# Starting layer 1's first chunk beside the last chunk of layer 0

## The chip, the cores and the metric

The kernel runs on one core of a Trainium2 chip. The metric is the device time of one execution in microseconds (us). The engines are TensorE (PE, with its weight loads PEld), VectorE (DVE), ScalarE (ACT), GpSimd (POOL) and SyncE (SP, which here only issues DMAs).

## The reference

Two layers work on x of 16 sequences x 256 tokens x 256 features, all in float32. Cut to what matters here:

```python
xn = layernorm(x)                             # layer 0
y  = recurrent_scan(xn) @ C + D * xn          # 32 complex states, along the tokens
z  = silu(gelu(xn @ proj1.T + b1) @ proj2.T + b2)
x  = x + y * z
xn = layernorm(x)                             # layer 1
q  = xn @ Wq                                  # 16 heads, 128 plain + 64 rotated features
kv = xn @ Wkv_a                               # 64 latent + 64 rotated features
c  = rmsnorm(kv[..., :64]) * kv_norm_w
k, v = split(c @ Wkv_b)                       # k is joined with the rotated part of kv
s  = causal_softmax(q @ k.T / sqrt(192)) @ v @ Wo
mid = (xn @ lora_A) * gate                    # 8 experts x 16; gate: softmax of the best two router logits
z  = silu(xn @ base_w.T + base_b + 2 * mid @ lora_B)
x  = x + s * z
```

## The kernel before

The 4,096 tokens are worked in 8 chunks of 512 tokens (two sequences); X[ch] stays on the chip through both layers. Layer 0 goes over all chunks first, then layer 1.

**Layer 0** is the loop `for ch in range(NCH)` (line 560). For each chunk: `hidden` (PE matmuls ph, ACT Gelu to hT), `recur` (PE pb, then a chain on DVE and POOL to hs), `norm0` and `turn0` of the next chunk (PE transposes tp, copies to xnT), `mix(ch, 0)` (32 matmuls pf, DVE add and ACT Silu to zf), `outs` (PE py, DVE dx), `finish0(ch, 0)` (POOL: dx times zf, then added to X), `mix(ch, 1)` and `finish0(ch, 1)` for the other half. In the last chunk there is no next chunk, so nothing stands between pb and the first pf. PSUM is held in pools `ps_mm` (4 buffers), `ps_y` (2) and `ps_f` (2).

**Layer 1** starts after the pools of layer 0 are given back (line 593); its own pools lie in the memory of layer 0, so an instruction that writes into them waits for the last user of the place. Its first steps, in lines 1002 to 1027, work on chunk 0:

- `norm_begin` and `norm_end` (lines 621 and 634): 4 bn_stats, 4 bn_aggr and one tensor_scalar on DVE, a power on POOL (rs), 4 tensor_scalar on DVE (xn).
- `transpose_chunk` (643): 8 PE transposes tp, 2 copies on ACT to xnT.
- `kv_begin`, `kv_end`, `key_chunk` (652 to 692): 8 matmuls pkv, an ACT Square, a chain on DVE and POOL (tmp, ss, rk, row), 4 transposes pk and a copy to kT, the keys.
- `router_chunk` (693): 8 matmuls pm, then some 20 small DVE operations (lg to gate) with one ACT Exp, and the gated product mid.
- the queries of the first two groups of four heads. `query_mm` makes pq on PE, `query_mul` multiplies the rotated part on DVE (qmul), `query_rot` adds it up on POOL (qrot), `query_move` sends it with 8 DMAs of SP to the query tile qg, `query_lat` writes the plain part to qg on ACT.

Then the loop over units (line 1033; one unit is a group of four heads of one sequence, 8 units to a chunk) writes `score_pack` (PE sc, DVE mask and maxima nm, ACT Exp to pr), `normalise` (DVE reciprocals sr, POOL product pr), `turn` and `send` (DVE transposes to turned, 4 DMAs to far), `fetch` (a DMA to pT), `values` (av), and among them the queries of later groups and the same steps norm to router for chunk ch + 1. The norm of the next chunk stands in units 0 and 2 of the chunk (lines 1096 and 1053).

The probabilities of a unit lie in one of two tiles `prs`, which are cleared at their making by two POOL memsets (lines 802 to 804).

Order: `pe` is a wrapper that keeps PE's instructions in the order of the text; in layer 1 so do `sp`, `ve`, `ac` and `gp` for the others. In layer 0 most DVE, ACT and POOL instructions are placed by the scheduler, with respect to data only. So the instructions of layer 1 may move ahead of instructions of layer 0, but not past each other: the norm of chunk 0, whose X is complete early, ran at 152.88 us on DVE.

The layer norm adds its scale to each instruction like this, which makes xn wait for rs of POOL:

```python
gp.tensor_tensor(k.rs, v, mhalf, ALU.pow)
...
    ve.tensor_scalar(
        k.xn[:, j, :], X[ch][:, j, :], k.mv[:, j, 0:1], k.rs[:, j : j + 1],
        ALU.subtract, ALU.mult,
    )
```

Of the kernel before, what the change touches and what calls it, by code (L numbers as in the profile page):

```python
# [40 lines left out]
def tile_two_layers(ctx: ExitStack, tc: tile.TileContext, d: dict, out: bass.AP):  # L41
# [153 lines left out]
    def bc_in(ap, n):  # L195

        return ap.unsqueeze(2).to_broadcast([ap.shape[0], ap.shape[1], n])


    with ExitStack() as l0:  # L200
# [359 lines left out]
        for ch in range(NCH):  # L560
            if ch > 1:
                hT = hidden(ch, xnT)
            if ch == 0:

                xnT2 = turn0(1, xn2)
                zf = [mix(ch, jp, hT) for jp in range(2)]
                hT = hidden(1, xnT2)
                turn_b()
                g = recur(ch, xnT)
                fold_heads(ch)  # L570
                g0_, xn0, zf0 = g, xn, zf
            else:
                g = recur(ch, xnT)
                if ch < NH // HG:
                    fold_heads(ch)
                if ch == 1:
                    zf = mix(ch, 0, hT)
                    dx = outs(0, g0_, xn0)
                    for jp in range(2):
                        finish0(0, jp, dx, zf0[jp])  # L580
                if ch + 1 < NCH:
                    xn2 = norm0(ch + 1)
                    xnT2 = turn0(ch + 1, xn2)
# [18 lines left out]

    sp = InOrder(nc.sync)
    ve = InOrder(nc.vector)
    ac = InOrder(nc.scalar)
    gp = InOrder(nc.gpsimd)
    ps_m1 = ctx.enter_context(tc.tile_pool(name="ps_m1", bufs=5, space=PSUM))
    ps_sc = ctx.enter_context(tc.tile_pool(name="ps_sc", bufs=3, space=PSUM))

    def m1(name, shape):  # L610
        return ps_m1.tile(shape, F32, tag="m1", name=name)

    class Chunk:
        pass

    chunks = [Chunk() for _ in range(NCH)]
    for k in chunks:
        k.attT, k.po = [], {}


    def norm_begin(ch):
        k = chunks[ch]
        st = sm.tile([P, TPC, 6], F32, tag="ln_st", name=f"st_1_{ch}")
        k.mv = sm.tile([P, TPC, 2], F32, tag="ln_mv", name=f"mv_1_{ch}")
        v = sm.tile([P, TPC], F32, tag="ln_ve", name=f"ve_1_{ch}")
        k.rs = sm.tile([P, TPC], F32, tag="ln_rs", name=f"rs_1_{ch}")
        for j in range(TPC):
            ve.bn_stats(st[:, j, :], X[ch][:, j, :])
        for j in range(TPC):
            ve.bn_aggr(k.mv[:, j, :], st[:, j, :])  # L630
        ve.tensor_scalar(v, k.mv[:, :, 1], LN_EPS, None, ALU.add)
        gp.tensor_tensor(k.rs, v, mhalf, ALU.pow)

    def norm_end(ch):
        k = chunks[ch]
        k.xn = x1.tile([P, TPC, D], F32, tag="xn", name=f"xn1_{ch}", bufs=1)
        for j in range(TPC):
            ve.tensor_scalar(
                k.xn[:, j, :], X[ch][:, j, :], k.mv[:, j, 0:1], k.rs[:, j : j + 1],
                ALU.subtract, ALU.mult,  # L640
            )

    def transpose_chunk(ch):
        k = chunks[ch]
        k.xnT = x1.tile([P, 2, CH], F32, tag="xnT", name=f"xnT1_{ch}")
        for c in range(2):
            ps = m1(f"tp_1_{ch}_{c}", [P, CH])
            for j in range(TPC):
                pe.transpose(ps[:, j * P : (j + 1) * P], k.xn[:, j, c * P : (c + 1) * P], ident)
            ac.copy(k.xnT[:, c, :], ps)  # L650

    def kv_begin(ch):

        k = chunks[ch]
        k.pkv = pkv = m1(f"pkv_{ch}", [P, TPC, P])
        for j in range(TPC):
            for c in range(2):
                pe.matmul(
                    pkv[:, j, :], k.xnT[:, c, j * P : (j + 1) * P], wkva[:, c, :],
                    start=(c == 0), stop=(c == 1),  # L660
                )
        k.row = a2.tile([P, TPC, P], F32, tag="row", name=f"row_{ch}")
        k.tmp = tmp = a2.tile([P, 3, TPC, KVL], F32, tag="tmp", name=f"tmp_{ch}", bufs=1)
        sq, ra, rb = tmp[:, 0], tmp[:, 1], tmp[:, 2]
        ss = sm.tile([P, TPC], F32, tag="ss", name=f"ss_{ch}")
        k.rk = sm.tile([P, TPC], F32, tag="rk", name=f"rk_{ch}")
        ac.activation(sq, pkv[:, :, 0:KVL], AF.Square)
        x1_ = pkv[:, :, KVL : KVL + HR]
        x2_ = pkv[:, :, KVL + HR : P]
        ve.tensor_tensor(ra[:, :, 0:HR], x1_, rope_k[:, 0], ALU.mult)  # L670
        ve.tensor_tensor(ra[:, :, HR:ROPE], x2_, rope_k[:, 0], ALU.mult)
        ve.tensor_tensor(rb[:, :, 0:HR], x2_, rope_k[:, 1], ALU.mult)
        ve.tensor_tensor(rb[:, :, HR:ROPE], x1_, rope_k[:, 2], ALU.mult)
        ve.tensor_reduce(ss, sq, AX.X, ALU.add)
        ve.tensor_scalar(ss, ss, 1.0 / KVL, RMS_EPS, ALU.mult, ALU.add)
        gp.tensor_tensor(k.rk, ss, mhalf, ALU.pow)
        gp.tensor_tensor(k.row[:, :, KVL:P], ra, rb, ALU.add)

    def kv_end(ch):
        k = chunks[ch]  # L680
        sq = k.tmp[:, 0]
        ve.tensor_tensor(sq, k.pkv[:, :, 0:KVL], bc_in(k.rk, KVL), ALU.mult)
        ve.tensor_tensor(k.row[:, :, 0:KVL], sq, bc(kvw_bc, TPC), ALU.mult)

    def key_chunk(ch):
        k = chunks[ch]
        pk = m1(f"pk_{ch}", [P, CH])
        for j in range(TPC):
            pe.transpose(pk[:, j * P : (j + 1) * P], k.row[:, j, :], ident)
        k.kT = a2.tile([P, CH], F32, tag="kT", name=f"kT_{ch}")  # L690
        ac.copy(k.kT, pk)

    def router_chunk(ch):

        k = chunks[ch]
        lg = sm.tile([P, TPC, NE], F32, tag="lg", name=f"lg_{ch}")
        mid = a2.tile([P, TPC, P], F32, tag="tmp", name=f"mid_{ch}", bufs=1)
        for jp in range(2):
            pm = m1(f"pm_{ch}_{jp}", [P, 2, 256])
            for j2 in range(2):  # L700
                j = 2 * jp + j2
                for c in range(2):
                    pe.matmul(
                        pm[:, j2, 0 : P + NE], k.xnT[:, c, j * P : (j + 1) * P], wmid[:, c, :],
                        start=(c == 0), stop=(c == 1),
                    )
            ve.tensor_tensor(
                lg[:, 2 * jp : 2 * jp + 2, :], pm[:, :, P : P + NE], bc(rb_bc, 2), ALU.add
            )
            ac.copy(mid[:, 2 * jp : 2 * jp + 2, :], pm[:, :, 0:P])  # L710

        def t3(name):
            return sm.tile([P, TPC, NE], F32, tag=name, name=f"{name}_{ch}")

        def t2(name):
            return sm.tile([P, TPC], F32, tag=name, name=f"{name}_{ch}")

        def first_max(l, n, between=None):

            m, fm, eq, oh = t2(f"m{n}"), t2(f"fm{n}"), t3(f"eq{n}"), t3(f"oh{n}")  # L720
            ve.tensor_reduce(m, l, AX.X, ALU.max)
            if between:
                between(m)
            ve.tensor_tensor(eq, l, bc_in(m, NE), ALU.is_equal)
            ve.tensor_tensor(eq, eq, desc, ALU.mult)
            ve.tensor_reduce(fm, eq, AX.X, ALU.max)
            ve.tensor_tensor(oh, desc, bc_in(fm, NE), ALU.is_equal)
            return m, oh

        ex = t3("ex")  # L730

        def exps(m):
            ve.tensor_tensor(ex, lg, bc_in(m, NE), ALU.subtract)
            ac.activation(ex, ex, AF.Exp)

        _, oh1 = first_max(lg, 1, exps)
        l2 = t3("l2")
        ve.scalar_tensor_tensor(l2, oh1, -3e38, lg, ALU.mult, ALU.add)
        _, oh2 = first_max(l2, 2)
        ve.tensor_tensor(oh1, oh1, oh2, ALU.add)  # L740
        ve.tensor_tensor(ex, ex, oh1, ALU.mult)
        sw = t2("sw")
        ve.tensor_reduce(sw, ex, AX.X, ALU.add)
        ve.reciprocal(sw, sw)
        ve.tensor_scalar(sw, sw, LORA_SCALE, None, ALU.mult)
        gate = t3("gate")
        ve.tensor_tensor(gate, ex, bc_in(sw, NE), ALU.mult)
# [451 lines left out]
```

## Time and profile before

| | us |
|---|---|
| median of 3 runs | 968.23 |
| lowest and highest of the runs | 966.02, 969.03 |
| the profiled execution | 970.78 |
| its span, first to last instruction | 969.0 |
| PE busy in the span | 934.6 |
| DVE, ACT, POOL busy | 617.5, 427.7, 421.5 |
| end of the last pf of layer 0 | 285.76 |
| first score matmul of layer 1 | 306.35 |

Lines of instructions have the start in us, the length in us, the engine, the line of the kernel (L52 is the wrapper's line, common to all that go through it), the operation, the tile written <- the tiles read, the shape and the count; in brackets the idle time of the engine before it and what ended it. Lines of waits have who waited for whom, the total in us, the times and the longest. Lines of stretches have the stretch, its length, the busy time of PE, PEld, DVE, ACT and POOL with instruction counts, the mean clock that was granted to PE (1.00 is full), the share and the rate of the DMAs.

### The profile page before, as it was taken

The page shows a single profiled execution, that of the slowest core. Times are in us where ns is not written, and L with a number is a line of the kernel's source. Part 1 is how long each engine was busy: PE and PEld are TensorE (multiplying, and loading weights), DVE is VectorE, ACT ScalarE, POOL GpSimd, SP SyncE. Part 2 cuts the span into 40 slices and gives each one's busy share as a digit, 9 for nine tenths or more (in the row PEclk, how much of TensorE's full clock was granted, in tenths as well). Part 3 has the DMA queues.
Part 4 walks back from the last instruction along what each step waited for, and adds up shares of the span by engine and source line. Part 5 has one row for each costly group of instructions (what it writes and reads, how often), then busy time and mean ns, then how long its engine had stood idle before and what let it go on. Part 6 is the DMA issues. An engine that isn't in the chain of part 4 may idle for free.

```text
span 969.0 us, 15714 instructions
## 1 busy us (share of the span) xinstructions
PE 934.6 (96%) x4762; PEld 670.7 (69%) x4762; DVE 617.5 (64%) x1942; ACT 427.7 (44%) x1422; POOL 421.5 (43%) x751
## 2 busy tenths in 40 slices
PE   4989999999999999999999999999999999999988
PEld 3847557756675566777777777777777776777776
DVE  6776415321236968867876786786788679677562
ACT  2331332233324546544554464555456455446540
POOL 3115334223233445553645455455446544546440
PEclk9989999999999989999999999999999999999999
DMA  9503000000002577777777677678667767867860
GB/s 312 173 5 105 0 1 1 1 0 1 1 0 37 121 199 186 208 189 188 190 186 201 168 169 224 158 191 202 171 166 210 201 171 183 209 166 190 221 192 29
DMA packets 195941, 133.90 MB, mean 138 GB/s; under 512 B 142160, under 2 KB 186512, under 8 KB 195856
## 3 DMA queue, kind: packets, MB, share of 16 engines
q1 hardware_dynamic: 192864, 127.18, 50.5%
q0 software_dynamic: 1376, 3.67, 1.0%
q10 hardware_dynamic: 1616, 2.04, 0.7%
q8 instruction: 39, 0.64, 0.3%
q14 instruction: 46, 0.38, 0.1%
HBM read 63.11 MB, written 52.95 MB: 120 GB/s over the span
## 4 chain that ended last, share of the span: by engine, by line
PE 87%; DVE 6%; POOL 2%; DMA 2%; ACT 1%; issue 1%; SPq 1%; ACTq 0%; POOLq 0%; DVEq 0%
PE pq L52 22%; PE sc L52 14%; PE po L52 10%; PE ph L52 10%; PE pf L52 9%; PE av L52 9%; PE pg L52 4%; PE pm L52 2%; PE pkv L52 1%; PE tp L52 1%; PE pb L52 1%; PE psq L52 1%; PE py L52 1%; DMA x<-in_x_dram 1%; SPq L52 1%
## 5 line engine op out<-in xcount | busy, mean ns | idle before, releaser
L52 ACT ACTIVATE pr<-sc,nm 128x256 f32<-128x256 f32 (+7 forms) x512 | 189.5, 380 | 287.3 <-DVE sr L52 197.4
L52 POOL TENSOR_SCALAR pr<-pr,sr 128x256 f32<-128x256 f32 (+7 forms) x512 | 192.2, 394 | 276.2 <-DVE sr L52 273.3
L52 PEld LDWEIGHTS sc<-kT,qg 128*128 128x128 f32 x1024 | 161.1, 192 | 64.5 <-issue 40.2
L52 PE MATMUL sc<-kT,qg 128*128 128x256 f32 (+7 forms) x1024 | 177.9, 308 | 6.1 <-DMA qg<-qrot 4.2
L52 DVE STREAM_TRANSPOSE turned<-pr 128x512 f32<-128x512 f32 x186 | 123.3, 688 | 15.1 <-POOL pr L52 14.9
L52 DVE TENSOR_REDUCE nm<-sc 128x1 f32<-128x256 f32 (+7 forms) x512 | 127.7, 301 | 6.6
L52 PE MATMUL pq<-xnT,wlat 128*128 128x512 f32 x256 | 124.4, 609 | 0.0
L52 PE MATMUL pq<-xnT,wrope 128*128 128x512 f32 x256 | 120.1, 592 | 0.0
L52 PE MATMUL ph<-xnT,p1T 128*128 128x512 f32 (+1 forms) x288 | 114.8, 558 | 3.6 <-ACT xnT L52 3.2
L52 PE MATMUL po<-wout,attT 128*128 128x256 f32 x512 | 115.8, 380 | 0.0
L52 PE MATMUL pf<-p2T,hT 128*128 128x256 f32 x512 | 113.9, 381 | 0.0
L52 PEld LDWEIGHTS po<-wout,attT 128*128 128x128 f32 x512 | 96.4, 190 | 20.9 <-issue 6.4
L52 PEld LDWEIGHTS pf<-p2T,hT 128*128 128x128 f32 x512 | 96.1, 190 | 15.5 <-issue 1.8
L52 ACT ACTIVATION_READ_ACCUMULATOR pr<-sc,nm 128x1 f32 x512 | 103.6, 202 | 0.0
L52 PEld LDWEIGHTS ph<-xnT,p1T 128*128 128x128 f32 x288 | 56.6, 197 | 57.4 <-issue 48.6
L52 PE MATMUL av<-pT,row 128*64 128x256 f32 (+1 forms) x1024 | 90.5, 329 | 0.5 <-DMA pT<-far 0.5
L52 POOL TENSOR_TENSOR qrot<-qmul,qmul 128x512 f32<-128x512 f32 x64 | 83.0, 1317 | 15.3 <-DVE sc L52 9.9
L52 DVE TENSOR_TENSOR qmul<-pq,rot_q 128x512 f32<-128x512 f32 x128 | 80.9, 674 | 0.0
L52 PEld LDWEIGHTS av<-pT,row 128*64 128x64 f32 x1024 | 64.2, 137 | 23.3 <-PE av L52 0.8
L52 DVE TENSOR_TENSOR sc<-sc,kmask 128x96 f32<-128x96 f32 (+1 forms) x192 | 45.9, 239 | 52.1 <-PE sc L52 50.7
L52 ACT ACTIVATE qg<-pq 64x512 f32<-64x512 f32 x128 | 75.4, 589 | 6.8 <-PE pq L52 6.0
L52 PEld LDWEIGHTS pq<-xnT,wlat 128*128 128x128 f32 x256 | 46.2, 193 | 32.2 <-issue 32.1
(166 smaller groups left out, 910.4 us busy)
## 6 DMA issues: line engine op xcount, KB each, us to landing
far<-turned SPq DMA_DIRECT2D x248, 192.0 KB, 3.6
pT<-far SPq DMA_DIRECT2D x62, 768.0 KB, 4.6
qg<-qrot SPq DMA_DIRECT2D x256, 64.0 KB, 2.3
x<-in_x_dram SPq DMA_DIRECT2D x7, 512.0 KB, 9.1
out_dram<-o POOLq DMA_DIRECT2D x28, 128.0 KB, 3.2
wqn<-in_wq_nopeT_dram SPq DMA_DIRECT2D x4, 512.0 KB, 5.2
wo<-in_Wo_dram SPq DMA_DIRECT2D x4, 512.0 KB, 5.3
p1T<-in_proj1T_dram ACTq DMA_DIRECT2D x2, 512.0 KB, 4.8
```

Source lines behind the costliest of these rows:

```text
L52: r = getattr(self.engine, name)(*args, **kw)
```

## The change

The definitions of layer 1's steps move ahead of layer 0, unchanged but for the pools that they take. The pools `sm1`, `x1` and a new `ak` (row, tmp, kT and mid) are opened in front of both layers and so share no memory with layer 0. `m1` takes PSUM from the pool in `place`: from `ps_mm` of layer 0 while the last chunk runs, from `ps_m1` afterwards. In the last chunk of layer 0 the steps of layer 1's chunk 0, and the norm of its chunk 1, are written between those of layer 0; they are taken out of the places where they stood.

```diff
+    sm1 = ctx.enter_context(tc.tile_pool(name="sm1", bufs=2))
+    x1 = ctx.enter_context(tc.tile_pool(name="x1", bufs=2))
+    ak = ctx.enter_context(tc.tile_pool(name="ak1", bufs=2))
...
+    place = {}
+
+    def m1(name, shape):
+        return place["pool"].tile(shape, F32, tag=place["tag"], name=name)
...
         for ch in range(NCH):
             if ch > 1:
                 hT = hidden(ch, xnT)
+            if ch == NCH - 1:
+                place.update(pool=ps_mm, tag="mm")
+                norm_begin(0)
+                norm_end(0)
...
+                last = ch == NCH - 1
+                if last:
+                    transpose_chunk(0)
+                    kv_begin(0)
                 if ch > 1:
                     zf = mix(ch, 0, hT)
+                if last:
+                    kv_end(0)
+                    key_chunk(0)
                 dx = outs(ch, g, xn)
                 finish0(ch, 0, dx, zf)
+                if last:
+                    router_chunk(0)
                 zf = mix(ch, 1, hT)
                 finish0(ch, 1, dx, zf)
+                if last:
+                    norm_begin(1)
+                    norm_end(1)
             xn, xnT = xn2, xnT2
...
-    sm = ctx.enter_context(tc.tile_pool(name="sm1", bufs=2))
-    x1 = ctx.enter_context(tc.tile_pool(name="x1", bufs=2))
+    place.update(
+        pool=ctx.enter_context(tc.tile_pool(name="ps_m1", bufs=5, space=PSUM)), tag="m1"
+    )
...
-    norm_begin(0)
-    norm_end(0)
     ve.tensor_scalar(bb_bc, bb_bc, 0.5, None, ALU.mult)
-    transpose_chunk(0)
-    kv_begin(0)
     query_mm(0, 0)
     query_mul(0, 0)
     query_mm(0, 1)
-    kv_end(0)
     query_mul(0, 1)
     query_rot(0)
     query_move(0)
-    key_chunk(0)
     query_mm(0, 2)
     query_lat(0, 2)
     query_mm(0, 3)
     query_lat(0, 3)
-    router_chunk(0)
...
-            if more:
+            if more and ch:
                 norm_end(ch + 1)
...
-        if r == 0 and more:
+        if r == 0 and more and ch:
             norm_begin(ch + 1)
```

More of the change, by code (lines that the diff above doesn't have):

```diff
@@ L197, in bc_in @@
         return ap.unsqueeze(2).to_broadcast([ap.shape[0], ap.shape[1], n])
+    sm1 = ctx.enter_context(tc.tile_pool(name="sm1", bufs=2))
+    x1 = ctx.enter_context(tc.tile_pool(name="x1", bufs=2))
+    ak = ctx.enter_context(tc.tile_pool(name="ak1", bufs=2))
+    sp = InOrder(nc.sync)
+    ve = InOrder(nc.vector)
+    ac = InOrder(nc.scalar)
+    gp = InOrder(nc.gpsimd)
+    place = {}
+    def m1(name, shape):
+        return place["pool"].tile(shape, F32, tag=place["tag"], name=name)
+    class Chunk:
+        pass
@@ new lines, in tile_two_layers, with norm_begin @@
+    chunks = [Chunk() for _ in range(NCH)]
+    for k in chunks:
+        k.attT, k.po = [], {}
+    def norm_begin(ch):
+        k = chunks[ch]
+        st = sm1.tile([P, TPC, 6], F32, tag="ln_st", name=f"st_1_{ch}")
+        k.mv = sm1.tile([P, TPC, 2], F32, tag="ln_mv", name=f"mv_1_{ch}")
+        v = sm1.tile([P, TPC], F32, tag="ln_ve", name=f"ve_1_{ch}")
+        k.rs = sm1.tile([P, TPC], F32, tag="ln_rs", name=f"rs_1_{ch}")
+        for j in range(TPC):
+            ve.bn_stats(st[:, j, :], X[ch][:, j, :])
+        for j in range(TPC):
+            ve.bn_aggr(k.mv[:, j, :], st[:, j, :])
+        ve.tensor_scalar(v, k.mv[:, :, 1], LN_EPS, None, ALU.add)
+        gp.tensor_tensor(k.rs, v, mhalf, ALU.pow)
@@ new lines, in norm_end, with transpose_chunk @@
+    def norm_end(ch):
+        k = chunks[ch]
+        k.xn = x1.tile([P, TPC, D], F32, tag="xn", name=f"xn1_{ch}", bufs=1)
+        for j in range(TPC):
+            ve.tensor_scalar(
+                k.xn[:, j, :], X[ch][:, j, :], k.mv[:, j, 0:1], k.rs[:, j : j + 1],
+                ALU.subtract, ALU.mult,
+            )
+    def transpose_chunk(ch):
+        k = chunks[ch]
+        k.xnT = x1.tile([P, 2, CH], F32, tag="xnT", name=f"xnT1_{ch}")
+        for c in range(2):
+            ps = m1(f"tp_1_{ch}_{c}", [P, CH])
+            for j in range(TPC):
+                pe.transpose(ps[:, j * P : (j + 1) * P], k.xn[:, j, c * P : (c + 1) * P], ident)
+            ac.copy(k.xnT[:, c, :], ps)
@@ new lines, in kv_begin @@
+    def kv_begin(ch):
+        k = chunks[ch]
+        k.pkv = pkv = m1(f"pkv_{ch}", [P, TPC, P])
+        for j in range(TPC):
+            for c in range(2):
+                pe.matmul(
+                    pkv[:, j, :], k.xnT[:, c, j * P : (j + 1) * P], wkva[:, c, :],
+                    start=(c == 0), stop=(c == 1),
+                )
+        k.row = ak.tile([P, TPC, P], F32, tag="row", name=f"row_{ch}")
+        k.tmp = tmp = ak.tile([P, 3, TPC, KVL], F32, tag="tmp", name=f"tmp_{ch}", bufs=1)
+        sq, ra, rb = tmp[:, 0], tmp[:, 1], tmp[:, 2]
+        ss = sm1.tile([P, TPC], F32, tag="ss", name=f"ss_{ch}")
+        k.rk = sm1.tile([P, TPC], F32, tag="rk", name=f"rk_{ch}")
+        ac.activation(sq, pkv[:, :, 0:KVL], AF.Square)
+        x1_ = pkv[:, :, KVL : KVL + HR]
+        x2_ = pkv[:, :, KVL + HR : P]
+        ve.tensor_tensor(ra[:, :, 0:HR], x1_, rope_k[:, 0], ALU.mult)
+        ve.tensor_tensor(ra[:, :, HR:ROPE], x2_, rope_k[:, 0], ALU.mult)
+        ve.tensor_tensor(rb[:, :, 0:HR], x2_, rope_k[:, 1], ALU.mult)
+        ve.tensor_tensor(rb[:, :, HR:ROPE], x1_, rope_k[:, 2], ALU.mult)
+        ve.tensor_reduce(ss, sq, AX.X, ALU.add)
+        ve.tensor_scalar(ss, ss, 1.0 / KVL, RMS_EPS, ALU.mult, ALU.add)
+        gp.tensor_tensor(k.rk, ss, mhalf, ALU.pow)
+        gp.tensor_tensor(k.row[:, :, KVL:P], ra, rb, ALU.add)
@@ new lines, in kv_end, with key_chunk @@
+    def kv_end(ch):
+        k = chunks[ch]
+        sq = k.tmp[:, 0]
+        ve.tensor_tensor(sq, k.pkv[:, :, 0:KVL], bc_in(k.rk, KVL), ALU.mult)
+        ve.tensor_tensor(k.row[:, :, 0:KVL], sq, bc(kvw_bc, TPC), ALU.mult)
+    def key_chunk(ch):
+        k = chunks[ch]
+        pk = m1(f"pk_{ch}", [P, CH])
+        for j in range(TPC):
+            pe.transpose(pk[:, j * P : (j + 1) * P], k.row[:, j, :], ident)
+        k.kT = ak.tile([P, CH], F32, tag="kT", name=f"kT_{ch}")
+        ac.copy(k.kT, pk)
@@ new lines, in router_chunk, with t3, t2, first_max @@
+    def router_chunk(ch):
+        k = chunks[ch]
+        lg = sm1.tile([P, TPC, NE], F32, tag="lg", name=f"lg_{ch}")
+        mid = ak.tile([P, TPC, P], F32, tag="tmp", name=f"mid_{ch}", bufs=1)
+        for jp in range(2):
+            pm = m1(f"pm_{ch}_{jp}", [P, 2, 256])
+            for j2 in range(2):
+                j = 2 * jp + j2
+                for c in range(2):
+                    pe.matmul(
+                        pm[:, j2, 0 : P + NE], k.xnT[:, c, j * P : (j + 1) * P], wmid[:, c, :],
+                        start=(c == 0), stop=(c == 1),
+                    )
+            ve.tensor_tensor(
+                lg[:, 2 * jp : 2 * jp + 2, :], pm[:, :, P : P + NE], bc(rb_bc, 2), ALU.add
+            )
+            ac.copy(mid[:, 2 * jp : 2 * jp + 2, :], pm[:, :, 0:P])
+        def t3(name):
+            return sm1.tile([P, TPC, NE], F32, tag=name, name=f"{name}_{ch}")
+        def t2(name):
+            return sm1.tile([P, TPC], F32, tag=name, name=f"{name}_{ch}")
+        def first_max(l, n, between=None):
+            m, fm, eq, oh = t2(f"m{n}"), t2(f"fm{n}"), t3(f"eq{n}"), t3(f"oh{n}")
+            ve.tensor_reduce(m, l, AX.X, ALU.max)
+            if between:
+                between(m)
+            ve.tensor_tensor(eq, l, bc_in(m, NE), ALU.is_equal)
+            ve.tensor_tensor(eq, eq, desc, ALU.mult)
+            ve.tensor_reduce(fm, eq, AX.X, ALU.max)
+            ve.tensor_tensor(oh, desc, bc_in(fm, NE), ALU.is_equal)
+            return m, oh
+        ex = t3("ex")
+        def exps(m):
+            ve.tensor_tensor(ex, lg, bc_in(m, NE), ALU.subtract)
+            ac.activation(ex, ex, AF.Exp)
+        _, oh1 = first_max(lg, 1, exps)
+        l2 = t3("l2")
+        ve.scalar_tensor_tensor(l2, oh1, -3e38, lg, ALU.mult, ALU.add)
+        _, oh2 = first_max(l2, 2)
+        ve.tensor_tensor(oh1, oh1, oh2, ALU.add)
+        ve.tensor_tensor(ex, ex, oh1, ALU.mult)
+        sw = t2("sw")
+        ve.tensor_reduce(sw, ex, AX.X, ALU.add)
+        ve.reciprocal(sw, sw)
+        ve.tensor_scalar(sw, sw, LORA_SCALE, None, ALU.mult)
+        gate = t3("gate")
+        ve.tensor_tensor(gate, ex, bc_in(sw, NE), ALU.mult)
+        m3 = mid.rearrange("p j (e r) -> p (j e) r", r=LR)
+        ve.tensor_tensor(m3, m3, bc_in(gate.rearrange("p j e -> p (j e)"), LR), ALU.mult)
+        k.mg = mid
@@ L583, in tile_two_layers @@
                     xnT2 = turn0(ch + 1, xn2)
+                last = ch == NCH - 1
+                if last:
+                    transpose_chunk(0)
+                    kv_begin(0)
                 if ch > 1:
                     zf = mix(ch, 0, hT)
+                if last:
+                    kv_end(0)
+                    key_chunk(0)
                 dx = outs(ch, g, xn)
                 finish0(ch, 0, dx, zf)
+                if last:
+                    router_chunk(0)
                 zf = mix(ch, 1, hT)
                 finish0(ch, 1, dx, zf)
+                if last:
+                    norm_begin(1)
+                    norm_end(1)
             xn, xnT = xn2, xnT2
-    sm = ctx.enter_context(tc.tile_pool(name="sm1", bufs=2))
-    x1 = ctx.enter_context(tc.tile_pool(name="x1", bufs=2))
+    place.update(
+        pool=ctx.enter_context(tc.tile_pool(name="ps_m1", bufs=5, space=PSUM)), tag="m1"
+    )
+    ps_sc = ctx.enter_context(tc.tile_pool(name="ps_sc", bufs=3, space=PSUM))
     qm = ctx.enter_context(tc.tile_pool(name="qm1", bufs=2))
@@ L601, in tile_two_layers @@
     dp = ctx.enter_context(tc.tile_pool(name="far1", bufs=3, space=bass.MemoryType.DRAM))
[L603 to L747, printed above, removed]
-        m3 = mid.rearrange("p j (e r) -> p (j e) r", r=LR)
-        ve.tensor_tensor(m3, m3, bc_in(gate.rearrange("p j e -> p (j e)"), LR), ALU.mult)
-        k.mg = mid
@@ L874, in score_pack @@
         if pi == 0:
-            u.nm = sm.tile([P, NQ], F32, tag="nm", name=f"nm_{u.n}", bufs=3)
-            u.sr = sm.tile([P, NQ], F32, tag="sr", name=f"sr_{u.n}", bufs=3)
+            u.nm = sm1.tile([P, NQ], F32, tag="nm", name=f"nm_{u.n}", bufs=3)
+            u.sr = sm1.tile([P, NQ], F32, tag="sr", name=f"sr_{u.n}", bufs=3)
         qg = groups[u.i // 2].qg
```

## The prediction, made before the result was known

> **What bounds the kernel now.** I read the page first (busy time, the 40 slices), then the list of waits, then the order-of-time rows where layer 0 hands over to layer 1.
>
> ```profile
> PE 934.6 (96%) x4762; PEld 670.7 (69%) x4762; DVE 617.5 (64%) x1942; ACT 427.7 (44%) x1422; POOL 421.5 (43%) x751
> PEclk9989999999999989999999999999999999999999
> ```
>
> TensorE (PE) is busy 934.6 of 969.0 us, so only its idle time and time at a lower clock can move the result. Slice 15 of the clock row (339 to 363 us) is below full clock. The waits of PE (total, times, longest) near the change are these:
>
> ```profile
> PE sc L52 <- DMA qg<-qrot: 4.2, 1, 4.2
> PE pk L52 <- DVE row L52: 1.8, 1, 1.8
> PE pkv L52 <- ACT xnT L52: 1.1, 2, 0.6
> ```
>
> The last two are what the moved steps cost in front of layer 1. The first is later, at 341.56. In order of time (start, us, engine):
>
> ```profile
> 285.76 1.04 PE L52 MATMUL tp<-ident,xn 128*128 128x128 f32 x8
> 285.99 2.69 POOL L804 MEMSET pr<- 128x1536 f32 x2 [2.74 <-PE pf L52]
> 288.65 1.27 POOL L497 TENSOR_TENSOR dx<-dx,zf 128x512 f32<-128x512 f32 x1
> 290.00 1.26 POOL L498 TENSOR_TENSOR x<-x,dx 128x512 f32<-128x512 f32 x1
> 295.45 0.63 PE L52 MATMUL pk<-ident,row 128*128 128x128 f32 x4 [1.82 <-DVE row L52]
> 296.47 2.48 POOL L52 TENSOR_TENSOR qrot<-qmul,qmul 128x512 f32<-128x512 f32 x2 [1.56 <-DVE qmul L52]
> 297.76 17.69 SPq L52 DMA_DIRECT2D qg<-qrot  x16
> 306.35 0.97 PE L52 MATMUL sc<-kT,qg 128*128 128x256 f32 x4
> ```
>
> The reader should see a second path beside PE: qmul on VectorE (DVE), qrot on GpSimd (POOL), eight DMAs on SP, then the first score sc. The last of the eight is issued at 302.57 and PE reaches sc at 306.35 without waiting: this path has almost no slack (the last issue needed 3.33 us to its sc at 341.56, which here would be 305.9). Later, PE does wait for such a DMA, and then runs at half clock (stretch, length, busy of PE; clock after POOL):
>
> ```profile
> 341.56 1.94 PE L52 MATMUL sc<-kT,qg 128*128 128x256 f32 x4 [4.20 <-DMA qg<-qrot]
> 342.00:346.00 4.00, 4.00 (x8) 2.17 (x8) 2.23 (x6) 0.99 (x4) 2.94 (x5) 0.50 0.92 327
> ```
>
> In the chain of waits the four sc take 1.94 instead of 0.82, four pq 3.41 instead of 1.72, six sc 1.27 instead of 0.82: 3.2 us lost after the 4.2.
>
> **Part 1, PE's own path to the first score.** No matmul is added or removed. The eight transposes tp and pkv move to the place of pf of the last chunk (270.58); pk, py and pm follow that pf. Before, tp to the next group took 290.03 - 285.76 = 4.27, with waits of 0.56 and 0.52 for the two copies of xnT. The second copy there stood behind a Silu; now the copies are adjacent: tp + 0.96 + 0.59 gives the first, 0.59 more the second, then 1.66 of pkv, 3.86 in all. So 0.41 is gained. The 1.82 of pk goes: row is made at about 280 on DVE, while pf runs to 281.55. PE would reach the first sc at 306.35 - 1.82 - 0.41 = 304.1.
>
> **Part 2, the path beside it.** In the changed program's order DVE runs, ahead of qmul: the routing, the norm statistics of chunk 1, three of its four xn, only then zf of the last half of layer 0, the fourth xn, bb_bc, qmul. POOL runs dx, x, both memsets of pr, then qrot; before, the memsets stood ahead of dx and ran while POOL was idle. Moved on PE: pf (7.11, as from 270.58 to py at 277.69) ends 270.58 + 3.86 + 7.11 = 281.55; pk 0.46, py 1.06, pm 1.85, each from its start to the next group's, give 284.9. The second lg starts 0.2 later (285.1), and routing took 306.24 - 301.40 = 4.84: 289.95. The norm is priced by chunk 0's, with idle POOL:
>
> ```profile
> 152.88 1.39 DVE L52 BATCH_NORM_STATS2 st<-x 128x6 f32<-128x256 f32 x4
> 155.94 1.38 DVE L52 TENSOR_SCALAR xn<-x,mv,rs 128x256 f32<-128x256 f32 x4 [1.18 <-POOL rs L52]
> ```
>
> From 152.88 to the end of the third xn is 4.05: 294.0. This is the wait that the change adds: xn waits for rs of POOL, and behind it on DVE stand zf, bb_bc and qmul; for zf wait ACT's Silu and POOL's dx. Then zf 0.63, a table load 1.28 (the exp of routing now lies between the two Silus), Silu 0.65 with gaps of 0.1: 296.7. dx and x took 2.61 (250.62 to 253.23): 299.3; memsets 2.66 (to dx at 288.65): 301.96; first half of qrot 1.3: 303.3. From the first issue to a possible sc is 305.9 - 297.76 = 8.15: 311.4. PE waits 311.4 - 304.1 = 7.3 us, and the first score starts **5.1 us later** than before, not 2.2 earlier. Bounds: xn at 0.59 each (the 2.36 of four at 326.24) gives +5.9; a landing 1 us faster (7.1, issue to landing 2.3 alone) +4.1.
>
> On the table load the Trainium skill, ScalarE: Activation LUTs, "What ACT_TABLE_LOAD costs", adds a drain of some 1.4 us to the 1.28; it speaks against this change. The rows show Silu 0.02 after the load's end at 279.91 and no such drain. By the page this path would be 1.4 longer and the forecast 1.4 higher; I take the row.
>
> **Part 3, the clock.** After 7.3 us of idling PE loses some 3.2, as at 341.56: **+3.2.** The stretches of 2 to 4 us there add up to 6.8 us at half clock, and to 3.4 at 934 (below); half of each, 3.4 and 1.7, are the bounds. The third table load (exp, 1.28, before the first pr) is on ACT; cover: the first sc buffer is wanted again 7.05 after the first sc, and its exp ended 4.2 after it.
>
> **Part 4, the second wait.** From the end of the sc group at 323.60 (324.42) DVE did mask, maxima, g, then xn of chunk 1 (2.28), transposes to 331.40; then SP four sends, eight issues, sc at 341.56: 17.14. PE got there in 12.94. Without xn: 14.86; without two small waits (0.21 for xn, 0.22 for pr): 12.5. The wait is **2.36 instead of 4.2**. POOL's three pr end at 328.43, when the transpose that needs them would start at 328.42: no more than that is gained. The statistics (1.9 at 314.20) are worth nothing: DVE had caught up at 324.45.
>
> Does the clock fall after 2.36? Rows speak for both: 1.82 idle at 293.63 left it at 1.00, 1.85 at 932.93 brought 0.70:
>
> ```profile
> PE pt L52 <- POOL pr L52: 3.2, 2, 1.9
> 934.00:936.00 2.00, 1.22 (x6) 1.22 (x7) 0.16 (x1) 1.06 (x5) 1.95 (x6) 0.70 0.96 304
> ```
>
> That stretch cost at most 1.7 (3.4 us at half). Being the longer wait, 2.36 is nearer the falling row: I take 1.2, ends 0 and 1.7. Before: 4.2 + 0.43 + 3.2 = 7.8; after: 2.36 + 1.2 = 3.6. **-4.3.**
>
> TensorE: Matmul & The Clock Gate, "Part 1: The HAM clock gate", puts the drop after one idle window of some 3.4 us; by it 2.36 would cost nothing more and the forecast would be 1.2 lower, while the row at 934 already differs from it.
>
> **Free parts.** Norm of chunk 0 moves within layer 0, where PE is busy 119.00 of 119.00 us from 106 to 225; uncovered it would cost 4.4. bb_bc (0.29) is in part 2's DVE queue, which qrot does not wait for last. Laying the pools out in front takes away the wait of tmp for x (2.98 on ACT), which is the 1.82 already counted. From 430 to 880 PE has no idle time, so a shift arrives at the end unchanged.
>
> **Sum.** +5.1 + 3.2 - 4.3 = **+4.0**. The profiled execution took 970.78 (span 969.0) and would take 974.8; it lies 2.55 above the median of 968.23, so the forecast is 968.23 + 4.0 = **972.2**.
>
> **Rivals.**
> - *The first score hardly waits (faster).* With nothing in the way qmul follows pq: pf ends 284.9 + 7.0 = 291.9, two pq 3.44, qmul 1.28: qrot at 296.7, and 1.3 + 8.15 later the score at 306.1, 0.2 earlier than before, after 2.0 of waiting (clock 1.2 as in part 4): -0.2 + 1.2 - 4.3 = -3.3: 964.9. For it: POOL is 43% busy, and the memsets need nothing of chunk 1. Against: POOL's and DVE's order. It decides if qrot starts before about 297 on this time scale (302 in part 2); each us later costs one, and from some 3 us of waiting the whole 3.2 of clock besides.
> - *The second wait vanishes, and the first costs one window of 3.4 us at half clock (no change).* 5.1 + 1.7 - 7.8 = -1.0: 967.2. It needs the third group's eight DMAs 2.4 us earlier than in part 4. Against: DVE, POOL and SP are all tight there.
> - *The second wait stays whole (slower still).* If SP's twelve issues (331.44 to 338.9) and not DVE set it, the 4.2 and its 3.2 remain: 5.1 + 3.2 = +8.3, 976.5. For: most of the chain from 334.47 to 338.85 is SP issuing. Against: its first send followed the DVE transpose by 0.04.
>
> **Numbers.** 0.3% is 2.9 us, about what a measurement of this kernel can tell from no change, so slower begins at 971.1. Forecast 0.53 (970.3 to 975), no change 0.23, slower still 0.13, faster 0.11. Of the forecast's share 0.08 lies below 971.1. Slower: 0.45 + 0.13 = 0.58; same 0.23 + 0.08 = 0.31; faster 0.11. The range goes from the no-change rival, less 1, to the slower one, plus 0.5: 966.2 to 977.0, which leaves out the faster case.
>
> **What would show it.** Right: the first sc waits some 7 us for DMA qg, with a clock of 0.5 after it; qrot starts after a memset; the pk wait is gone; the wait of the third group's first sc is 2 to 3 us. Wrong: memsets ahead of dx, a first sc without a wait, or a second wait still over 4.

## The result, and the profile after

The changed kernel takes 979.00 us (median of 6 runs, 976.81 to 980.96) where the kernel before, beside it, takes 967.75: a ratio of 1.0116, 95% interval 1.0099 to 1.0133, or 11.25 us more. The prediction was 972.2 us, with a range up to 977.0: slower, as forecast, by almost three times as much. The profiled execution of after took 979.33 us, span 977.6.

First the page of after (busy time; the clock in 40 slices of 24.4 us), then its list of the waits of PE:

```profile
PE 935.6 (96%) x4762; PEld 670.1 (69%) x4762; DVE 619.2 (63%) x1942; ACT 430.6 (44%) x1424; POOL 421.2 (43%) x751
PEclk9979899999998999999999999999999999999999
```

```profile
PE sc L52 <- DMA qg<-qrot: 11.4, 2, 8.1
...
PE ph L52 <- ACT hT L577: 4.3, 1, 4.3
...
PE pkv L52 <- ACT xnT L52: 0.2, 1, 0.2
```

The first line holds what was predicted in kind: two waits of sc, 8.1 and 3.2 (predicted: 7.3 and 2.36). The wait of pk is gone and that of pkv is 0.2. But ph waits 4.3 us for hT, where the kernel before waits 0.4, and the clock row has a dip in its fifth slice (98 to 122 us) that the row of before lacks: far inside layer 0, some 170 us ahead of the first step that the change was meant to touch. In order of time, DVE and PE of **before** there:

```profile
94.03 4.35 DVE L174 TENSOR_SCALAR xn<-x,mv,rs 128x256 f32<-128x256 f32 x4 [5.14 <-POOL dx L489]
...
98.91 0.69 DVE L470 TENSOR_TENSOR zf<-pf,b_bc 128x512 f32<-128x512 f32 x1
```

```profile
102.38 7.13 PE L52 MATMUL ph<-xnT,p1T 128*128 128x512 f32 x16 [0.43 <-ACT hT L424]
109.44 1.08 PE L52 MATMUL pb<-xnT,bT 128*64 128x256 f32 x8
```

and of **after**:

```profile
92.51 4.36 DVE L174 TENSOR_SCALAR xn<-x,mv,rs 128x256 f32<-128x256 f32 x4 [3.09 <-POOL dx L642]
96.79 0.41 DVE L52 BATCH_NORM_STATS2 st<-x 128x6 f32<-128x256 f32 x1
...
97.77 0.37 DVE L52 BATCH_NORM_AGGREGATE mv<-st 128x2 f32<-128x6 f32 x4
98.17 0.17 DVE L52 TENSOR_SCALAR ve<-mv 128x4 f32<-128x4 f32 x1
99.97 1.38 DVE L52 TENSOR_SCALAR xn<-x,mv,rs 128x256 f32<-128x256 f32 x4 [1.63 <-POOL rs L52]
101.27 0.68 DVE L623 TENSOR_TENSOR zf<-pf,b_bc 128x512 f32<-128x512 f32 x1
```

```profile
104.73 9.97 PE L52 MATMUL ph<-xnT,p1T 128*128 128x512 f32 x16 [4.29 <-ACT hT L577]
114.63 1.08 PE L52 MATMUL pb<-xnT,bT 128*64 128x256 f32 x8
```

The rows marked L52 on DVE are layer 1's norm of chunk 0 (two of its four statistics ran earlier, at 87.47). They stand in front of a zf of layer 0's second chunk, and xn of that norm waits 1.63 for rs of POOL. Behind zf stand ACT's Silu, a table load and the Gelu hT, which PE waits for. After is 1.52 ahead at 92.51 and 2.36 behind at zf: 3.9 us. Then ph runs for 9.90 to the next group instead of 7.06, the clock being halved after the wait: 2.8 us more.

The hand-over to layer 1, by DVE, ACT, POOL, SP and PE:

```profile
299.96 0.68 DVE L623 TENSOR_TENSOR zf<-pf,b_bc 128x512 f32<-128x512 f32 x1
```

```profile
300.72 1.28 ACT L624 ACT_TABLE_LOAD   x1 [8.68 <-DVE zf L623]
302.02 0.63 ACT L624 ACTIVATE zf<-zf 128x512 f32<-128x512 f32 x1
```

```profile
302.72 1.27 POOL L650 TENSOR_TENSOR dx<-dx,zf 128x512 f32<-128x512 f32 x1 [3.77 <-ACT zf L624]
304.07 1.26 POOL L651 TENSOR_TENSOR x<-x,dx 128x512 f32<-128x512 f32 x1
305.40 2.69 POOL L826 MEMSET pr<- 128x1536 f32 x2
308.06 2.48 POOL L52 TENSOR_TENSOR qrot<-qmul,qmul 128x512 f32<-128x512 f32 x2
```

```profile
309.35 14.16 SPq L52 DMA_DIRECT2D qg<-qrot  x16
```

```profile
316.95 1.94 PE L52 MATMUL sc<-kT,qg 128*128 128x256 f32 x4 [8.14 <-DMA qg<-qrot]
...
352.33 1.46 PE L52 MATMUL sc<-kT,qg 128*128 128x256 f32 x4 [3.22 <-DMA qg<-qrot]
```

This is part 2's chain, link by link: zf, table load, Silu, dx, x, two memsets, qrot, DMA, sc. The first score starts 10.6 us later than in before (306.35), of which 5.2 come from layer 0 (pb of the last chunk: 274.76 against 269.57), so 5.4 from here. The last row is the second wait, 3.22 instead of 4.20.

### The profile page after: what moved, and what is told of

Its sections match the earlier page's. It is cut to its first block, busy times and chain, and to the rows that moved or that the text cites. A ratio compares the mean times of both kernels' runs of the same rounds, so it can differ in the third digit from the quotient of the medians.

```text
span 977.6 us, 15724 instructions
## 1 busy us (share of the span) xinstructions
PE 935.6 (96%) x4762; PEld 670.1 (69%) x4762; DVE 619.2 (63%) x1942; ACT 430.6 (44%) x1424; POOL 421.2 (43%) x751
## 4 chain that ended last, share of the span: by engine, by line
PE 81%; DVE 7%; POOL 4%; DMA 3%; issue 2%; SPq 2%; ACT 1%; POOLq 0%; DVEq 0%; ACTq 0%
PE pq L52 19%; PE sc L52 13%; PE ph L52 10%; PE po L52 10%; PE pf L52 9%; PE av L52 8%; PE pg L52 4%; SPq L52 2%; PE pm L52 1%; PE pkv L52 1%; POOL pr L52 1%; DMA far<-turned 1%; PE tp L52 1%; PE pb L52 1%; PE psq L52 1%
## 5 line engine op out<-in xcount | busy, mean ns | idle before, releaser
L52 ACT ACTIVATE pr<-sc,nm 128x256 f32<-128x256 f32 (+7 forms) x512 | 189.5, 380 | 280.6 <-DVE sr L52 198.0
L52 POOL TENSOR_SCALAR pr<-pr,sr 128x256 f32<-128x256 f32 (+7 forms) x512 | 192.5, 395 | 278.0 <-DVE sr L52 271.5
L52 PEld LDWEIGHTS sc<-kT,qg 128*128 128x128 f32 x1024 | 159.6, 191 | 72.0 <-issue 48.5
L52 PE MATMUL sc<-kT,qg 128*128 128x256 f32 (+7 forms) x1024 | 177.1, 307 | 13.2 <-DMA qg<-qrot 11.4
L52 DVE STREAM_TRANSPOSE turned<-pr 128x512 f32<-128x512 f32 x186 | 123.3, 688 | 15.3 <-POOL pr L52 15.0
L52 DVE TENSOR_REDUCE nm<-sc 128x1 f32<-128x256 f32 (+7 forms) x512 | 127.6, 301 | 6.6
L52 PE MATMUL pq<-xnT,wlat 128*128 128x512 f32 x256 | 125.3, 613 | 0.0
L52 PE MATMUL ph<-xnT,p1T 128*128 128x512 f32 (+1 forms) x288 | 117.2, 567 | 7.4 <-ACT hT L577 4.3
L52 PE MATMUL pq<-xnT,wrope 128*128 128x512 f32 x256 | 120.1, 592 | 0.0
L52 PE MATMUL po<-wout,attT 128*128 128x256 f32 x512 | 115.8, 380 | 0.0
L52 PE MATMUL pf<-p2T,hT 128*128 128x256 f32 x512 | 113.7, 380 | 0.0
L52 PEld LDWEIGHTS po<-wout,attT 128*128 128x128 f32 x512 | 96.4, 190 | 20.9 <-issue 6.4
L52 PEld LDWEIGHTS pf<-p2T,hT 128*128 128x128 f32 x512 | 96.1, 190 | 14.8 <-issue 1.4
L52 ACT ACTIVATION_READ_ACCUMULATOR pr<-sc,nm 128x1 f32 x512 | 103.5, 202 | 0.0
L52 PEld LDWEIGHTS ph<-xnT,p1T 128*128 128x128 f32 x288 | 57.4, 200 | 62.8 <-issue 50.5
L52 PE MATMUL av<-pT,row 128*64 128x256 f32 (+1 forms) x1024 | 90.5, 329 | 0.6 <-DMA pT<-far 0.6
L52 POOL TENSOR_TENSOR qrot<-qmul,qmul 128x512 f32<-128x512 f32 x64 | 82.5, 1310 | 10.6 <-DMA qg<-qrot 10.6
L52 DVE TENSOR_TENSOR qmul<-pq,rot_q 128x512 f32<-128x512 f32 x128 | 80.7, 673 | 7.0 <-POOL qrot L52 7.0
L52 DVE TENSOR_TENSOR sc<-sc,kmask 128x96 f32<-128x96 f32 (+1 forms) x192 | 45.9, 239 | 58.7 <-PE sc L52 57.2
L52 PEld LDWEIGHTS av<-pT,row 128*64 128x64 f32 x1024 | 64.2, 137 | 23.3 <-PE av L52 0.8
L52 ACT ACTIVATE qg<-pq 64x512 f32<-64x512 f32 x128 | 75.4, 589 | 5.6 <-PE pq L52 4.8
L52 PEld LDWEIGHTS pq<-xnT,wlat 128*128 128x128 f32 x256 | 46.8, 195 | 33.2 <-issue 33.1
```

The lines of the kernel that those rows point to most:

```text
L52: r = getattr(self.engine, name)(*args, **kw)
```

## The experiments

Each kernel was timed beside the kernel before, whose median was 966.9 (first four), 968.82 (next four) and 967.61 (last two). The interval in brackets belongs to the measured ratio; the quotient of the two medians can differ from that ratio by up to 0.1%, about 1 us. Differences in us are those of the medians unless said otherwise. Times inside one trace are compared as lengths: profiled executions differ by up to 2.7 us already at the ph near 100 us.

**1. The norm of chunk 0 put late.** In the changed kernel, the instruction of DVE that the norm must follow is named:

```diff
+            hm[ch] = nc.vector.tensor_tensor(h, g, ct, ALU.mult).ins    # hs, in recur
...
                 place.update(pool=ps_mm, tag="mm")
+                ve.last = hm[3]
                 norm_begin(0)
```

> The changed kernel, with one order added: the norm of layer 1's first chunk is put on DVE behind hs of layer 0's fourth chunk, where it stood before (152.88 us). Everything else of the change stays. Theory A (the separate pools let this norm run on DVE in front of a zf of layer 0's second chunk, where PE then waits 4.3 us for hT and runs some 6.8 us at half clock): that wait falls back to 0.4, the clock stays full from 94 to 114 us, and 979.0 - 3.9 - 2.8 = 972.3 us. Theory B (the norm costs nothing in layer 0, all 11 us are lost at the hand-over): 979 us, the wait for hT unchanged or moved elsewhere.

Measured: 971.47 us, ratio 1.0057 (1.0037 to 1.0077). Its waits:

```profile
PE sc L52 <- DMA qg<-qrot: 11.5, 3, 8.1
...
PE ph L52 <- ACT hT L577: 0.4, 1, 0.4
```

The wait for hT is 0.4, the clock stays full between the start-up and the hand-over, and the waits of sc are what they were. Theory A holds: the loss against the kernel before falls from 11.25 us to 4.6 (5.5 by the ratio), so some 6 to 7 us of it came from the place of one norm in layer 0; the traces give 3.9 of wait and 2.8 of clock.

**2. Only the pools.** The kernel before with `sm1`, `x1` and `ak` opened in front of both layers, no step moved:

```diff
+    sm1 = ctx.enter_context(tc.tile_pool(name="sm1", bufs=2))
+    x1 = ctx.enter_context(tc.tile_pool(name="x1", bufs=2))
+    ak = ctx.enter_context(tc.tile_pool(name="ak1", bufs=2))
```

> The kernel before, with nothing of the change but the pools laid out in front of both layers: every step of layer 1 stands where it stood. Theory A: its norm of chunk 0 goes early as in the changed kernel, hT is waited for some 4.3 us at 100 to 105 us, the clock halves behind it, so 967.8 + 6.7 = 974.5 us, less up to 1.8 if the wait of pk goes with the shared memory: 972.7 to 974.5. Theory B: 967.8 us, or 966 with the wait of pk gone.

Measured: 975.27 us, ratio 1.0089 (1.0074 to 1.0104).

```profile
PE ph L52 <- ACT hT L577: 4.5, 1, 4.5
PE sc L52 <- DMA qg<-qrot: 4.2, 1, 4.2
...
PE pk L52 <- DVE row L52: 1.9, 1, 1.9
```

The norm goes early by the pools alone. No step of the kernel before was moved, so it was the memory shared with layer 0 that held the norm back; which tile of layer 0 held the place was not looked up. With pools of their own the statistics wait only for X of chunk 0, and the scheduler puts the norm between two instructions of layer 0 on DVE. The wait (4.05 more) and the clock behind it (2.7) make 6.7 of the 8.4 us; the rest is not accounted for. The wait of pk stayed, though its supposed cause went: ACT began tmp 0.03 after the end of pkv (294.69), where before it had begun 1.1 after it, behind x. What took its place is on POOL: the memsets of pr, which before ran ahead of dx, now ran behind x (295.04, 2.69 long), and both ss on DVE (1.41 instead of 0.17, to 297.76) and rk on POOL (297.84) came out only as they ended.

**3. The norm of chunk 1 back in the loop of units.**

```diff
-                if last:
-                    norm_begin(1)
-                    norm_end(1)
...
-            if more and ch:
+            if more:
                 norm_end(ch + 1)
...
-        if r == 0 and more and ch:
+        if r == 0 and more:
             norm_begin(ch + 1)
```

> The changed kernel with the norm of chunk 1 put back into layer 1's loop (statistics in unit 0, xn in unit 2). Theory A (this norm holds the zf of layer 0's last half, and with it POOL's dx, x, memsets and qrot): first score 4.0 us earlier, its wait 8.1 - 4.0 = 4.1; the second wait grows from 3.3 by the 2.3 of xn to 5.6 and its clock loss from 1.9 to 3.2: 979.0 - 4.0 + 3.6 = 978.6 us. Theory C (POOL or SP hold the first score by something else): first wait still 8, 982.6 us.

Measured: 978.87 us, ratio 1.0124 (1.0109 to 1.014): nothing gained on the whole, as expected. PE and DVE:

```profile
312.96 1.94 PE L52 MATMUL sc<-kT,qg 128*128 128x256 f32 x4 [5.02 <-DMA qg<-qrot]
...
350.56 1.05 PE L52 MATMUL sc<-kT,qg 128*128 128x256 f32 x4 [4.23 <-DMA qg<-qrot]
```

```profile
295.97 0.69 DVE L623 TENSOR_TENSOR zf<-pf,b_bc 128x512 f32<-128x512 f32 x1 [0.58 <-PE pf L52]
```

The first wait falls by 3.1 and not by 4.0, since zf now waits for the end of pf itself; the second is back at 4.2 (5.6 was expected). This step moves a wait from one place to the other.

**4. The memsets behind qrot.**

```diff
-    for t in prs:
-        nc.gpsimd.memset(t, 0.0)
...
     query_rot(0)
+    for t in prs:
+        gp.memset(t, 0.0)
```

> The changed kernel with the two memsets of pr behind the first qrot on POOL instead of ahead of it. Theory A: qrot starts 2.7 us earlier, the first wait is 8.1 - 2.7 = 5.4 us, the rest as it was: 979.0 - 2.7 = 976.3 us. Theory C (the DMAs' landing is set by something else than qrot): wait of 8, 979 us; if the memsets then hold the first pr, later still.

Measured: 975.88 us, ratio 1.0095 (1.0077 to 1.0113). On POOL qrot follows x at once, and the first wait is 5.4:

```profile
302.62 1.26 POOL L651 TENSOR_TENSOR x<-x,dx 128x512 f32<-128x512 f32 x1
303.85 2.48 POOL L52 TENSOR_TENSOR qrot<-qmul,qmul 128x512 f32<-128x512 f32 x2
306.27 2.69 POOL L52 MEMSET pr<- 128x1536 f32 x2
```

```profile
312.75 1.94 PE L52 MATMUL sc<-kT,qg 128*128 128x256 f32 x4 [5.38 <-DMA qg<-qrot]
```

**5. The hand-over made light.** Edits 1 and 4, and the norm of chunk 1 behind group 1's products:

```diff
-                if last:
-                    norm_begin(1)
-                    norm_end(1)
...
     query_mul(1, 1)
+    norm_begin(1)
+    norm_end(1)
```

> The changed kernel with three edits: norm of chunk 0 behind hs of the fourth chunk (as in the first run), the memsets of pr behind the first qrot, and the norm of chunk 1 behind group 1's qmul instead of in front of the zf of layer 0's last half. The moved transposes, keys and routing stay in the last chunk. Theory A (DVE's norm and POOL's memsets are what delays the first score): zf right behind routing, qrot some 6 us earlier than in the first run, first wait 1.8 to 2.5 instead of 8.1, with 0 to 2 of clock behind it; the second wait as there, 3.2. Against the kernel before: first score -0.9, clock +1.2, second wait 5.1 instead of 7.8: -2.4, about 964.5 us. Theory D (the moved routing itself, its table load and its DVE time, costs the most): first wait still 5 or more, 968 us or more.

Measured: 966.73 us, ratio 0.9983 (0.9973 to 0.9994): 2.1 us under the kernel before, where the changed kernel is 11.25 over it, with all of its moved transposes, keys and routing kept. The first wait:

```profile
304.19 1.57 PE L52 MATMUL sc<-kT,qg 128*128 128x256 f32 x4 [2.29 <-DMA qg<-qrot]
```

So the moved work as such was not the loss; most of it was what stood in front of the two zf and of qrot. Theory D falls. The second wait stays, at 3.44.

**6. The routing back as well.**

```diff
-                if last:
-                    router_chunk(0)
...
     query_lat(0, 3)
+    router_chunk(0)
```

> The kernel of the run before, with the routing of chunk 0 put back behind the first group's queries; only the transposes, keys and the norm stay beside layer 0. Theory A: no table load between the two Silus and no routing in front of qmul; qrot's DMAs land when PE has done pm and seven pq: no first wait, the first score 2.2 to 2.7 us earlier than in the kernel before, second wait 3.2 with 1.9 of clock (5.1 instead of 7.8): -4.9 to -5.4, about 962 us. Theory D: the same 962, but then the run before is at 968 or more. Neither: a first wait of over 2.

Measured: 971.39 us, ratio 1.0029 (1.0019 to 1.0038), where 962 was expected. The first score did come without a wait, but a new wait took its place. PE's waits, then DVE and ACT:

```profile
PE pg L52 <- ACT mT L52: 5.5, 1, 5.5
```

```profile
301.19 2.48 DVE L52 TENSOR_TENSOR qmul<-pq,rot_q 128x512 f32<-128x512 f32 x4
303.59 1.40 DVE L52 BATCH_NORM_STATS2 st<-x 128x6 f32<-128x256 f32 x4
...
306.60 3.26 DVE L52 TENSOR_SCALAR xn<-x,mv,rs 128x256 f32<-128x256 f32 x4 [1.13 <-POOL rs L52]
309.77 0.22 DVE L52 TENSOR_TENSOR sc<-sc,kmask 128x64 f32<-128x64 f32 x1
```

```profile
310.87 0.47 ACT L52 ACTIVATE pr<-sc,nm 128x256 f32<-128x256 f32 x1 [8.17 <-DVE nm L52]
...
311.76 0.58 ACT L52 COPY mT<-pmT 128x512 f32<-128x512 f32 x1
```

The first score was made at 301.3. Its mask waits on DVE until 309.77, behind qmul and the norm of chunk 1; ACT keeps its order, so mT stands behind the first two exps that wait for that mask, and PE waits for mT. In run 5 the score itself was late (304.19) and covered most of the norm: the mask came at 307.63, and pg did not wait. That it is the norm and not the late routing is argued here from the rows; run 10 tests it.

**7 and 8. The third group's DMAs ahead of the sends**, in run 6's kernel and, alone, in the kernel before:

```diff
+        if i == 2:
+            query_move(n)
         if w:
             if here:
                 turn_here(w, 0)
             else:
                 turn(w, 0)
                 send(w)
         if not odd:
-            if n is not None:
+            if n is not None and i != 2:
                 query_move(n)
```

> The kernel of the run before, with the third group's eight DMAs of qrot issued ahead of unit 1's four sends on SP, once, in unit 2. Theory E (the second wait is SP's order: qrot is ready at 330.4 in the first run while SP stands idle until the send at 334.0, and the eight follow only at 336.3): the DMAs start some 5.8 us earlier, the second wait of 3.2 and its 1.9 of clock go: 962 - 5.1 = 957 us. Theory F (the prediction's: the path through DVE's transposes sets it): 962 us, the wait stays near 3.

> The kernel before, with nothing changed but the third group's eight DMAs ahead of unit 1's four sends on SP in unit 2. Theory E: qrot is ready at 327.4, SP idle until 331.4; the wait of 4.2 and the 3.2 of clock behind it go: 967 - 7.4 = 959.6 us. Theory F: 967 us, the wait stays.

Measured: 969.78 us, ratio 1.0018 (1.0005 to 1.0031), 1.6 less than run 6 where 5.1 less was expected, and the two intervals overlap; and 964.13 us, ratio 0.9959 (0.9945 to 0.9973), 4.7 less than before by the medians, 4.0 by the ratio, where 7.4 was expected. SP of the kernel before, and of run 8:

```profile
331.44 2.22 SPq L52 DMA_DIRECT2D far<-turned  x4
333.76 5.77 SPq L52 DMA_DIRECT2D qg<-qrot  x8
```

```profile
325.34 6.52 SPq L52 DMA_DIRECT2D qg<-qrot  x8
331.96 2.48 SPq L52 DMA_DIRECT2D far<-turned  x4
```

and PE's waits in run 8, where the line of sc for qg is gone:

```profile
PE sc L52 <- ACT pr L52: 4.0, 4, 2.0
...
PE av L52 <- DMA pT<-far: 1.9, 1, 1.9
```

Theory E holds for the wait: the eight DMAs had nothing to wait for but their place in SP's queue (qrot ended at 327.45 in before, the eight began at 333.76). Of the 7.4 us expected in run 8, 3.5 come back as later waits: 2.1 more for pr and 1.4 more for pT, whose transfers now start later. In run 7 the wait of 3.21 and the half clock behind it are gone too; a wait of 1.7 for a later group's qg and 1.4 more for pT stand further on.

**9 and 10. Two versions with this order**: run 5's kernel with it, and a kernel that moves only chunk 0's norm (late), transposes and keys, with routing and the norm of chunk 1 at their old places, the memsets behind qrot and the new order on SP.

> The run with the lightened hand-over (norm of chunk 0 late, memsets behind qrot, norm of chunk 1 behind group 1's qmul, routing beside layer 0), and the third group's DMAs ahead of unit 1's sends. If the second wait is SP's order in this kernel too, its 3.44 and some 1.9 of clock go, and, as in the kernel before with the same edit, about 3.4 comes back as waits for pT and pr further on: a gain of 2 to 3.5, ratio to the kernel before 0.995 to 0.997. If the two edits contend (the DMAs late again behind DVE's norm): 0.998 as without.

> Of the change only the norm of chunk 0 (put late), its transposes and its keys stay beside layer 0; routing and the norm of chunk 1 are back at their old places, the memsets stand behind the first qrot, and the third group's DMAs go ahead of unit 1's sends. Theory G (the norm of chunk 1 in front of the first mask on DVE is what made PE wait 5.5 us for mT when routing was put back): no such wait, the first score 2.7 us earlier than in the kernel before, and the gain of the DMAs' order of 4.0 kept: -6.7, ratio 0.993. Against G (it is the late routing, mid and its copy mT behind qmul, that pg waits for): a wait of 4 or more for mT, ratio 0.997 or above.

Measured: 965.4 us, ratio 0.9976 (0.9962 to 0.999), a miss: it is nearer to the 0.998 of no gain than to the 0.995 to 0.997 expected, and the interval holds values of both. The wait of 3.44 did go, so the DMAs were not late there; 2.09 for pT and 2.17 for a later group's qg stand further on. And **961.88 us, ratio 0.9946 (0.9929 to 0.9962)**, faster than both kernels. The waits of PE after the start, in the tenth:

```profile
PE sc L52 <- ACT pr L52: 3.9, 4, 1.8
PE pt L52 <- POOL pr L52: 3.4, 2, 1.9
PE ph L52 <- ACT xnT L52: 3.2, 1, 3.2
PE av L52 <- DMA pT<-far: 2.6, 2, 2.0
```

No wait for mT (theory G holds), none for qg, and the clock is full from the start-up to the last microsecond. Expected was 0.993, inside the interval. What the moved transposes and keys add to the order on SP is not clear of the noise: run 8, with the order alone, is at 0.9959, and the two intervals overlap.

## Why the prediction was right and wrong

| step | predicted | in the traces |
|---|---|---|
| norm of chunk 0 in layer 0: wait, clock | 0 | +3.9, +2.8 |
| first score later, by the hand-over | +5.1 | +5.4 |
| clock behind it | +3.2 | +2.6 |
| second wait and its clock | -4.3 | -2.8 |
| sum | +4.0 | +11.9 |
| median | | +11.25 |

The spans of the two profiled executions differ by 8.6 only: before's reached the ph of the second chunk 1.5 later (94.92 against 93.41), and at 934.8 it had 3.4 us of half clock behind a wait of 1.85 for pr, which after's had at full clock (1.7 us). Both lie outside the change.

- **The failed step is "Free parts": "Norm of chunk 0 moves within layer 0, where PE is busy 119.00 of 119.00 us from 106 to 225; uncovered it would cost 4.4."** The cover was read around the norm's old place at 153 us. That place came from the memory the norm shared with layer 0, and the change takes this sharing away; the new place, at 97 us, lies ahead of the stretch that was read and has no cover. The norm was priced at nothing, and cost 3.9 of wait and 2.8 of clock. The price named for the uncovered case, 4.4, was near the 3.9; the clock behind the wait was not in it. Run 1 takes the step back and lands at +4.6 (+5.5 by the ratio) against a forecast of +4.0; run 2 makes it alone. A second sentence there was wrong without moving the sum, that laying the pools out takes away the wait of pk: in run 2 tmp no longer waits for x, yet pk waits 1.89, since the memsets had moved in front of rk.
- **Part 1** held: on the time scale of before PE would have reached the first score at 316.95 - 8.14 - 5.19 = 303.6 (304.1 predicted). Most of the 0.5 is the group of tp and pkv, which took 3.49; the 3.86 put down for it is also more than its own terms, 0.96 + 0.59 + 0.59 + 1.66 = 3.80.
- **Part 2** held as a mechanism and in its sum: the score at 311.8 on that scale (311.4). Two terms missed in opposite ways: routing took 6.05 from the second lg to st (4.84 predicted), since one of its small products took 1.21 us; the way from the first issue to sc took 7.60 (8.15). Runs 3, 4 and 5 show norm, memsets and both together as links of it. On the table load, the rows of after agree with the choice that was made: Silu at 302.02, directly behind the load that began at 300.72 and took 1.28.
- **Part 3**: 2.6 instead of 3.2, inside its bounds, but in part by luck: the half clock lasted 10.2 us (311.9 to 322.1) and not 6.8, and half of it lay in the wait itself, where it costs nothing.
- **Part 4** is mis-sized by 1.5. Its path was right (14.7 from sc to sc, 14.86 predicted), but PE got there sooner, in 11.5 and not 12.5 (0.6 of it: the transposes of chunk 1 took 0.90, not 1.5, when xn was ready). So the wait was 3.2 and not 2.36, and its clock 1.8 and not 1.2. What set the path was SP's order behind DVE's transposes, as runs 7 and 8 show.
- **The rivals**: "the first score hardly waits" named DVE's and POOL's order as what speaks against it, and run 5, which takes the two out of the way, gives a wait of 2.3. "The second wait stays whole" named SP's twelve issues: the wait did not stay whole, as DVE's transposes still set when the sends start, but that the eight DMAs stand behind the sends on SP is what runs 7 and 8 show. None of the rivals had a mechanism in layer 0.

## What to carry to other kernels

When tiles get pools of their own, ask which instructions were held back by the shared memory: a scheduler that places by data will pull them forward, into whatever stands there, so read the new order of every engine at the new place and price the cover there. A step moved beside other work is paid by the first thing queued behind it on its engine; a norm of one chunk cost 6.7 us in front of one zf, nothing in front of another, and a wait of 5.5 in front of a mask. And where an engine waits for a DMA, look at whether its data was ready and its queue idle: the order of two groups of issues on SP alone was worth 4.0 us here; run 10, which adds the moved keys, gained 5.2 (both by the ratio), and the difference is not clear of the noise.

## What the runs showed of the hardware

- **DVE beside POOL.** Four xn took 1.38 us with POOL idle (99.97 in after) and 3.26 beside qrot (306.60 in run 6; qrot on POOL from 306.53 to 309.06). The slow product of routing (290.86 to 292.07 in after) stood beside x of POOL (290.76, 1.27) and took 1.21 instead of 0.19. The Trainium skill, SBUF — State Buffer, "SBUF: two separate sides", says that these two engines share a pair of ports by an exclusive lock: a DVE instruction with two inputs in SBUF, as this product has, and a POOL instruction that reads SBUF cannot hold it together, and the one that starts later blocks until the other's instruction is over. The product, which ends as x ends, agrees.
- **The clock after a wait.** Every wait of PE of 2.27 us or more in layer 1 and at the hT of layer 0's second chunk brought half clock: 3.4 us of it with 2.3 to 3.4 (6.8 with the 3.21 of run 6), 6.8 with 4.2 to 5.5 (3.4 with the 4.23 of run 3), and 10.2 with 8.1. What falls inside the wait itself costs nothing. Of the 40 waits of 1.5 to 2.2 us behind 80 us in the twelve traces, 34 left the clock full; six (1.96 in run 9, 2.02 in run 4, and the 1.85 of pt between 926 and 945 us in before and runs 2, 4 and 9) were followed by 3.4 us at half. The same wait of pt left it full in the other eight traces, at 1.85 to 1.87, so its length alone does not decide. The rule of the page that the prediction names (TensorE: Matmul & The Clock Gate, "Part 1: The HAM clock gate"), read as one wholly idle window of some 3.4 us, is contradicted by the 2.27 and the 2.29 of runs 9 and 5.
- **A grid of 3.41 us.** In each trace the granted clock changes only at times that lie whole multiples of 3.41 us apart: in after at 103.65, 110.48, 311.86, 322.10, 352.82 and 356.24. Adding up PE's idle time between neighbouring times of this grid, from 80 us to 15 us before the end in all twelve traces, gives this: from full clock, an interval with 2.02 us of idle or more was always followed by half, one with 1.53 or less never, and those between went both ways; from half clock, an interval with 0.57 or less was always followed by full, one with 0.68 or more never. Thus in run 9 the 2.17 at 356.46, cut into 1.36 and 0.81, left the clock full, and the 2.27 at 304.11, inside one interval, did not. What decides between 1.53 and 2.02 is open.
